# A graph network's third layer: the transposes and the projection of a group moved from two rounds to three rounds behind its sums

## The chip, the cores and the metric

The kernel runs on one core of one Trainium2 chip. The metric is the device time of one execution in microseconds; it was 6518.21 us before the change (median of 3 runs, 6515.67 to 6524.41). A core has several engines that work beside each other: TensorE (PE; its weight loads are PEld), VectorE (DVE), ScalarE (ACT), GpSimd (POOL) and SyncE (SP). Here SP issues most of the plain transfers and POOL issues the gathers.

## The reference, cut to what matters

There are 12500 nodes with 256 features each and 200000 edges, sorted by their target. Three layers of a graph network come first, then a layer norm, an attention over the same edges, and another layer norm.

```python
def _sage_layer(x, src, dst, inv_deg, W_self, W_neigh, b):
    agg = jax.ops.segment_sum(x[src], dst, num_segments=N_NODES)
    mean = agg * inv_deg[:, None]
    return x @ W_self + mean @ W_neigh + b
h = relu(_sage_layer(features, ...)); h = relu(_sage_layer(h, ...)); h = _sage_layer(h, ...)
x = _layernorm(x + h)                       # the end of the third layer: called z below
ZU = jnp.einsum('nd,kdr->knr', Z, U)        # the projection of z onto 4 heads of 16
# attention along the edges over ZU, one gradient step, relu
x = _layernorm(x + _L1_gnn_ref(x, ...))
```

The third layer differs from the first two: its rows are normalised, and each block of rows is also transposed (`zT`) and projected onto 64 columns (`zu`), since the attention reads `z`, its transpose and its projection.

## The kernel before

**Two ways of summing.** Most target nodes get their sums group by group. A group is 1792 edges; 76 groups in the third layer cover the first 8404 nodes. The rows of the sources are gathered into `xg` (14 gathers by POOL, line 838), split into a high and a low part in `hl` (ScalarE, line 858; VectorE, line 860), and multiplied on TensorE with a one-hot matrix `oh` (line 866). A further matmul (line 469) adds the sum carried over from the group before. The last 4096 nodes get their sums from a dense product instead: a matrix of edge counts (`c`, cast by ScalarE at line 749) with all rows (`hz`), in 392 steps of 8 matmuls 128x512 each (line 755, into `px`). Blocks of these nodes are ended in `end_block`. The dense steps are dealt out over the groups' rounds as `units`; about 5.7 fall to a round.

**A group's seven steps.** `group(g)` (line 820) is a Python generator, and each `next` writes out one step:

1. loads, gathers, one-hot matrix, the first half of the sums
2. the second half of the sums and the carry
3. the mean (ScalarE, line 908)
4. transposes of the own rows `hb` and of `mean` into `pT`, copied to `hT` (line 368)
5. eight products into `pO` (line 354) and `sage_end`: bias (line 344), residual (348), the layer norm (334 to 339), which writes `hn`. VectorE does all of it but one square root on ScalarE (337)
6. in the third layer alone, in `finish`: two transposes of `hn` into `pT` (line 363), copied to `zT` (368)
7. the projection into `pO` (line 374), its copy `zu` (376), a square and two small reductions for a bound (672 to 675), and three stores by SP of `zu`, `hn` and `zT` (line 440)

**What sets the order.** Lines 927 to 959 lay the steps out in rounds. A round has seven turns, `turns`: the newest group takes steps 1 and 2 in turns 2 and 5 (counted from 0), the group before it takes steps 3, 4 and 5 in turns 0, 3 and 6, and in the third layer the one before that, `old[0]`, takes steps 6 and 7 in turns 1 and 4. The dense units are spread between the turns. `chained` ties the matmul groups in that order: the first of a group comes after the last of the group before it. The matmuls between the first and the last of a group are not tied so, and a planner, which orders each engine's instructions, may place them earlier. The engines then take their instructions in the planned order.

So step 5 of a group is the last turn of one round, and step 6 of the same group is the second turn of the next round.

**Buffers.** `hn` has 3 buffers, `zT` 4, `xg` 3, `hl` 2, `c32` 3, `hz` 3, and `pT` and `pO` are one PSUM tile each, shared by all their users. `hn` is held from step 5 until its store in step 7.

Of the kernel before, what the change touches and what calls it, by code (L numbers as in the profile page):

```python
# [9 lines left out]
F32 = mybir.dt.float32  # L10
# [13 lines left out]
P = 128  # L24
# [24 lines left out]
def tile_gnn_resnorm(  # L49
# [14 lines left out]
    N, D = x.shape  # L64
# [7 lines left out]
    L = len(w_self)  # L72
# [115 lines left out]
    with tc.tile_pool(name="prep", bufs=1) as prep, \  # L188
# [78 lines left out]
        far = prep.tile([P, NG * GT], F32, name="far")  # L267
# [73 lines left out]
    def sage_end(wk, l, wts, po, hn, xb):  # L341

        n = po.shape[0]
        nc.vector.tensor_add(po, wts[2][:n], po)  # L344
        if l < L - 1:
            return nc.scalar.activation(hn, po, AF.Relu)
        y = wk.tile([n, D], F32, name="y")
        nc.vector.tensor_add(y, xb, po)
        return layernorm(wk, y, hn)
# [121 lines left out]
    def fast_sage():  # L471
        with ExitStack() as fx:
# [82 lines left out]
            def chained(first, last):  # L555
                if chain[0] is not None:
                    after(chain[0], first)
                chain[0] = last
# [4 lines left out]
            def count_ends(pool, n):  # L563
                for g in ends_of[counted[0]:n]:
                    row_ends(pool, g)
                    counted[0] += 1
# [214 lines left out]
            def due(l, g):  # L781
                sg, ahead = (SG, 0) if l else (SG0, G1)
                n, end = NDL[l] // sg * NQ, swept(l)
                if g >= end:
                    k = cuts[NDL[l]].NGS - LAG - end
                    return n + (2, 2, 4)[l] * sg * min(k, g + 1 - end) // k
                if l:
                    return n * (g + 1) // end

                n1 = n * 3 // 5  # L790
                return max(0, n1 * (g + 1 - G1) // (GB - G1) if g < GB else n - (n - n1) * (end - g - 1) // (end - GB))

            def built(g):
                if g < GA:
                    return max(0, g + 4 - GA)
                if g < G1:
                    return 3 + PER * (g + 1 - GA) // (G1 - GA)
                return min(BUILDS, 3 + PER + (BUILDS - PER - 3) * (g + 1 - G1) // (GB - G1))

            turn, H, summed = 0, GT // 2, []  # L800
            for l in range(L):
                table = x if l == 0 else hd[l - 1]
                W = (D + 2, D, D)[l]
                cut = cuts[NDL[l]]
# [3 lines left out]
                with ExitStack() as lx:  # L808
                    done, formed = 0, 0
                    lk = lx.enter_context(tc.tile_pool(name="layer", bufs=2))  # L810
# [9 lines left out]
                    def group(g):  # L820
# [94 lines left out]
                        yield  # L915
                        po, *mm = sage_products(ps, wts[l], hT)
                        chained(*mm)
                        hn = lk.tile([P, D], F32, name="hn", bufs=3)
                        sage_end(lk, l, wts[l], po, hn, xb)
                        tiles, made = yield from finish(l, lk, ps, hn, po, light)  # L920
                        store_rows(tiles, at[0], made, at[1])
# [2 lines left out]

                    live, rounds = [], 2 if l < L - 1 else 3
                    for g in range(cut.NGS + rounds - 1):
                        units, old = [], list(live)
                        if g < cut.NGS:  # L930
                            new = group(g)
                            live.append(new)
                            todo, more = due(l, g) - done, built(g) - formed if l == 0 else 0
                            done, formed = done + todo, formed + more
                            n = max(todo, more)
                            for i in range(n):
                                units += [forming] * ((i + 1) * more // n - i * more // n)
                                units += [steps_] * ((i + 1) * todo // n - i * todo // n)

                        late = old.pop() if old and g <= cut.NGS else None  # L940
                        turns = [late, old[0] if old else None, new if g < cut.NGS else None, late,
                                 old[0] if old else None, new if g < cut.NGS else None, late]
                        assert len(old) < 2
                        n = len(turns)
                        for i in range(n):
                            if turns[i] is not None:
                                next(turns[i])
                            if i == 2 and l == 0 and g < cut.NGS:

                                soon = min(NU, 1 + max(0, built(g + 1) - 3 + PER - 1) // PER) if built(g + 1) else 0  # L950
                                count_ends(tk, max(counted[0] + (1 if soon else needs[U0] // 2),
                                                   max((needs[u] for u in parts[:soon]), default=0)))
                                for _ in range(-(-NQ // ZB // (G1 - 2))):
                                    next(xsplit, None)
                            for u in units[len(units) * i // n:len(units) * (i + 1) // n]:
                                next(u, None)
                        if g >= rounds - 1:
                            live.pop(0)
                    assert not live
                    assert next(steps_, None) is None and (l or (next(forming, 0) == 0 and next(xsplit, 0) == 0))  # L960

            t1 = wp.tile([P, 1], F32, name="t1")
# [282 lines left out]
    with tc.If(ok > 0) as which:  # L1245
        fast_sage()
# [38 lines left out]
```

## Time and profile before

| what | value |
|---|---|
| median of 3 runs | 6518.21 us |
| the profiled execution: own time, span | 8272.62 us, 8270.8 us |
| busy in the span: PE, PEld, DVE, ACT, POOL | 5557.8, 4432.6, 3901.5, 3473.0, 4811.3 us |
| mean granted TensorE clock | 0.763 |
| first layer until about | 2290 us |
| second layer, first and last mean (line 908) | 2307.9, 3958.6 us |
| third layer, first and last mean | 4055.1, 5952.2 us |
| attention, from about | 5970 us to the end |

The profiled execution is an execution of its own and took 1754 us longer than the median. Times in the profile are counted from the first instruction. A line of groups or of the timeline names the line in the kernel, the engine, the operation, what is written and read, and how often; the idle time stands behind it, with what ended it. "remote" stands for a releaser that the profile could not name. Ends of matmuls are modelled.

### The profile page before, as it was taken

The page shows a single profiled execution, that of the slowest core. Times are in us where ns is not written, and L with a number is a line of the kernel's source. Part 1 is how long each engine was busy: PE and PEld are TensorE (multiplying, and loading weights), DVE is VectorE, ACT ScalarE, POOL GpSimd, SP SyncE. Part 2 cuts the span into 40 slices and gives each one's busy share as a digit, 9 for nine tenths or more (in the row PEclk, how much of TensorE's full clock was granted, in tenths as well). Part 3 has the DMA queues.
Part 4 walks back from the last instruction along what each step waited for, and adds up shares of the span by engine and source line. Part 5 has one row for each costly group of instructions (what it writes and reads, how often), then busy time and mean ns, then how long its engine had stood idle before and what let it go on. Part 6 is the DMA issues. An engine that isn't in the chain of part 4 may idle for free. (4 is left out here: it accounts for less than half of the span.)

```text
span 8270.8 us, 86872 instructions
## 1 busy us (share of the span) xinstructions
PE 5557.8 (67%) x23570; PEld 4432.6 (54%) x23570; DVE 3901.5 (47%) x9939; ACT 3473.0 (42%) x6309; POOL 4811.3 (58%) x4977
## 2 busy tenths in 40 slices
PE   4678787777678888887577777777544444444445
PEld 3556566555556666666465656566434333443344
DVE  4655545433434444444344545444445555555555
ACT  2333333344345454444344444444334444444444
POOL 5555555555566565565455555545366666666665
PEclk7888888888889998898788888889755555555555
DMA  7766666766566666665466656666333333333332
GB/s 207 244 203 217 220 225 223 226 214 218 178 195 217 208 214 207 206 213 178 156 190 184 192 178 191 185 181 195 108 86 88 88 94 88 88 89 88 91 91 67
DMA packets 896774, 1391.65 MB, mean 168 GB/s; under 512 B 191216, under 2 KB 540424, under 8 KB 892173
## 3 DMA queue, kind: packets, MB, share of 16 engines
q1 hardware_dynamic: 650511, 834.50, 31.3%
q0 software_dynamic: 213152, 496.65, 21.5%
q10 hardware_dynamic: 32606, 54.81, 1.9%
q8 instruction: 189, 3.10, 0.2%
q14 instruction: 316, 2.59, 0.1%
HBM read 1175.15 MB, written 210.33 MB: 168 GB/s over the span
## 5 line engine op out<-in xcount | busy, mean ns | idle before, releaser
L121 POOL DMA_INDIRECT xg<-h_d,srcI x2128 | 2082.3, 979 | 1645.5 <-issue 604.6
L755 PE MATMUL px<-c,hz 128*128 128x512 f32 x8232 | 2405.2, 433 | 266.6 <-issue 128.7
L121 POOL DMA_INDIRECT zs<-zu_d,srcI x1563 | 1495.9, 957 | 828.2 <-issue 416.8
L755 PEld LDWEIGHTS px<-c,hz 128*128 128x128 f32 x8232 | 1613.2, 203 | 646.0 <-issue 178.6
L749 ACT ACTIVATE c<-c 128x1024 fp32r<-128x1024 uint8 (+1 forms) x1274 | 1123.0, 893 | 1891.3 <-remote 692.8
L121 POOL DMA_INDIRECT xg<-in_x_dram,srcI x1218 | 1170.4, 961 | 925.0 <-PE pA L874 450.9
L462 DVE TENSOR_TENSOR oh<-rel,gconst 128x1792 fp32r<-128x1792 f32 (+1 forms) x354 | 714.2, 2018 | 1098.8 <-PE pO L382 312.1
L860 DVE TENSOR_TENSOR hl<-xg,hl 128x256 fp32r<-128x256 f32 x2128 | 780.2, 420 | 539.1 <-ACT hl L858 434.2
L1057 PE MATMUL pT<-ident,ag 128*64 128x128 f32 x112 | 47.2, 422 | 1157.3 <-DVE ag L392 625.5
L858 ACT ACTIVATE hl<-xg 128x512 fp32r<-128x512 f32 x1216 | 622.8, 569 | 266.3 <-PE pA L866 88.0
L1057 PEld LDWEIGHTS pT<-ident,ag 128*64 128x64 f32 x112 | 14.4, 129 | 1238.2 <-DVE ag L392 669.9
L866 PE MATMUL pA<-hl,oh 128*128 128x512 f32 x2128 | 625.3, 430 | 53.3 <-issue 51.0
L866 PEld LDWEIGHTS pA<-hl,oh 128*128 128x128 f32 x2128 | 432.9, 206 | 163.4 <-issue 59.8
L874 PE MATMUL pA<-xg,oh 128*128 128x258 f32 x1764 | 511.1, 451 | 3.8 <-DMA b<-in_L_gnn_b_dram 2.6
L874 PEld LDWEIGHTS pA<-xg,oh 128*128 128x128 f32 x1764 | 402.1, 233 | 94.7 <-issue 15.5
L645 ACT ACTIVATE win<-pc 128x392 uint16<-128x392 f32 x512 | 240.9, 495 | 459.6 <-PE pc L642 204.6
L344 DVE TENSOR_TENSOR pO<-b,pO 128x256 f32<-128x256 f32 x306 | 130.9, 428 | 639.8 <-remote 484.6
L354 PE MATMUL pO<-ws,hT 128*128 128x256 f32 x968 | 284.2, 419 | 171.4 <-DVE hs L661 50.5
L1027 DVE TENSOR_TENSOR zz<-zs,pD 128x896 f32<-128x896 f32 x224 | 242.2, 1082 | 328.7 <-remote 159.7
L1019 PE MATMUL pD<-z,ohT 128*128 128x128 f32 x1563 | 360.9, 418 | 53.3 <-DVE lg L1030 18.4
L633 DVE TENSOR_SCALAR oa<-iota,kt 128x128 bf16<-128x128 f16 x1024 | 268.9, 263 | 244.8 <-remote 86.6
L1019 PEld LDWEIGHTS pD<-z,ohT 128*128 128x128 f32 x1563 | 346.9, 333 | 54.1 <-issue 35.5
(257 smaller groups left out, 8112.4 us busy)
## 6 DMA issues: line engine op xcount, KB each, us to landing
hz<-hs_d SPq DMA_DIRECT2D x637, 512.0 KB
c<-cnt_d SPq DMA_DIRECT2D x112, 896.0 KB
ohT<-rel_d SPq DMA_DIRECT2D x111, 896.0 KB
hs_d<-hs SPq DMA_DIRECT2D x218, 256.0 KB
cnt_d<-win ACTq DMA_DIRECT2D x32, 1568.0 KB
xg<-h_d,srcI POOLq DMA_INDIRECT x2128
c<-cnt_d SPq DMA_DIRECT2D x70, 448.0 KB
zs<-zu_d,srcI POOLq DMA_INDIRECT x1563
```

Source lines behind the costliest of these rows:

```text
L121: return nc.gpsimd.indirect_dma_start(out=dst_ap, out_offset=None, in_=table, in_offset=bass.IndirectOffsetOnAxis(ap=idx, axis=0))
L354: mm = [nc.tensor.matmul(po, hT[:, i], wts[i // DC][:, i % DC], start=i == 0, stop=i == 2 * DC - 1) for i in range(2 * DC)]
L462: nc.vector.tensor_tensor(oh[:, :m], r[:, :m].unsqueeze(2).to_broadcast([P, m, P]), nodes.unsqueeze(1).to_broadcast([P, m, P]), op=op)
L633: nc.vector.tensor_scalar(oa[:, c], iota16[:, :P], kt[:, 0, at], None, op0=OP.is_equal)
L749: nc.scalar.activation(c32.rearrange("p (k d) -> p k d", d=P), c8[:, :, b % CB], AF.Copy)
L755: made.append(nc.tensor.matmul(px[f][i], hz[:, b % ZB, a:a + P].bitcast(F32R), c32[:, i * 512:(i + 1) * 512], start=b == 0 and part == 0, ...
L858: nc.scalar.activation(hi[:, b + j:b + j + n, :W], xg[:, a + j:a + j + n, :W], AF.Copy)
L860: nc.vector.tensor_tensor(lo[:, b + j, :D], xg[:, a + j, :D], hf[:, b + j, :D], op=OP.subtract)
L866: mm.append(nc.tensor.matmul(pa, oh[:, a + j], hl[:, j].rearrange("p i d -> p (i d)"), start=first, stop=stop))
L874: mm.append(nc.tensor.matmul(pa[:, :W], oh[:, a + j], xg[:, a + j, :W], start=first, stop=stop))
L1019: mm = [nc.tensor.matmul(pd[:, j * 2 * KR:(j + 1) * 2 * KR], ohT[:, a + j], z2.rearrange("p k i r -> p (k i r)"), start=True, stop=True) f ...
L1027: nc.vector.tensor_mul(zz, zg.unsqueeze(2).to_broadcast([P, n * K, 2, R]), pd[:, :n * 2 * KR].rearrange("p (m i r) -> p m i r", i=2, r=R))
```

## The change

In the third layer step 6 and step 7 are taken by the group three rounds behind the newest instead of two; `hn` gets a fourth buffer, as it is held one round longer. The list `live` now keeps all groups, and `late`, `far` and `now` are picked from it by number. The number of rounds stays: in the last round the two groups that are left take steps 6 and 7 one after the other. In the first two layers `far` is None, as `old[0]` was, and the turns come out as before.

```diff
-                        hn = lk.tile([P, D], F32, name="hn", bufs=3)
+                        hn = lk.tile([P, D], F32, name="hn", bufs=4)
...
-                    live, rounds = [], 2 if l < L - 1 else 3
-                    for g in range(cut.NGS + rounds - 1):
-                        units, old = [], list(live)
+                    live, lag = [], 1 if l < L - 1 else 3
+                    for g in range(cut.NGS + min(lag, 2)):
+                        units = []
                         if g < cut.NGS:
-                            new = group(g)
-                            live.append(new)
+                            live.append(group(g))
...
-                        late = old.pop() if old and g <= cut.NGS else None
-                        turns = [late, old[0] if old else None, new if g < cut.NGS else None, late,
-                                 old[0] if old else None, new if g < cut.NGS else None, late]
-                        assert len(old) < 2
+                        late = live[g - 1] if 0 < g <= cut.NGS else None
+                        far = live[g - lag] if l == L - 1 and g >= lag else None
+                        now = live[g] if g < cut.NGS else None
+                        turns = [late, far, now, late, far, now, late]
+                        if g > cut.NGS:
+                            turns = [far, far, live[-1], live[-1]]
                         n = len(turns)
...
-                        if g >= rounds - 1:
-                            live.pop(0)
-                    assert not live
+                    assert all(next(s, 0) == 0 for s in live)
```

## The prediction

> **What bounds the kernel now.** The change touches the third layer alone, so I first read the windows table for the second layer's and third layer's steady stretches (columns: stretch, length, then busy us and instructions of PE, PEld, DVE, ACT, POOL; then granted clock, DMA share, GB/s).
>
> ```profile
> 2330.00:3990.00 1660.00, 1364.06 (x5527) 1078.40 (x5526) 702.71 (x1629) 812.35 (x1390) 984.98 (x1010) 0.90 0.66 206
> 4075.00:5806.00 1731.00, 1316.10 (x5692) 1054.76 (x5693) 798.66 (x2155) 754.35 (x1265) 918.04 (x935) 0.88 0.62 186
> ```
>
> TensorE is busiest in both: 82% and 76%; POOL is at 53% and DMA at 62% in the third. Then the waits of the third layer (who waits for whom: us in total, times, longest) and its row for the transposes of `hn`:
>
> ```profile
> POOL xg L121 <- ACT hl L858: 459.9, 51, 16.8
> PE pT L363 <- DVE hn L339: 280.4, 36, 13.2
> ACT c L749 <- remote: 274.0, 43, 13.5
> DVE pO L344 <- remote: 273.5, 31, 11.9
> ```
>
> ```profile
> L363 PE MATMUL pT<-ident,hn 128*128 128x128 f32 x138 | 37.9, 367 | 304.0 <-DVE hn L339 280.4 <-DVE bn_rs L338 11.6 <-issue 11.1
> ```
>
> So 304 us of TensorE idleness end at the instruction that is moved. The timeline says how much of it the move can remove. First a common round (start, length, what; idle before it in brackets):
>
> ```profile
> 4712.91 1.03 PE L354 MATMUL pO<-wn,hT 128*128 128x256 f32 x4
> 4713.59 3.54 PE L755 MATMUL px<-c,hz 128*128 128x512 f32 x14
> 4714.08 1.42 DVE L860 TENSOR_TENSOR hl<-xg,hl 128x256 fp32r<-128x256 f32 x4
> 4715.42 0.42 DVE L344 TENSOR_TENSOR pO<-b,pO 128x256 f32<-128x256 f32 x1
> ...
> 4718.01 0.57 DVE L339 TENSOR_SCALAR hn<-y,bn_mv,bn_rs 128x256 f32<-128x256 f32 x1
> ...
> 4718.73 0.41 PE L363 MATMUL pT<-ident,hn 128*128 128x128 f32 x2 [0.69 <-DVE hn L339]
> ```
>
> The products end at 4713.94. VectorE is still in its L860 subtractions and takes up L344 1.48 us later; L344 to the end of L339 is 3.16. TensorE has 4.09 us of other matmuls and then idles 0.69. Now the other kind of round:
>
> ```profile
> 4807.91 1.03 PE L354 MATMUL pO<-wn,hT 128*128 128x256 f32 x4
> 4808.59 3.55 PE L755 MATMUL px<-c,hz 128*128 128x512 f32 x14
> ...
> 4819.27 0.43 DVE L344 TENSOR_TENSOR pO<-b,pO 128x256 f32<-128x256 f32 x1 [10.24 <-remote]
> ...
> 4822.34 0.69 PE L363 MATMUL pT<-ident,hn 128*128 128x128 f32 x2 [9.51 <-DVE hn L339]
> ```
>
> L344 waits for nothing but the products (and its queue), recorded as done at 4808.9, and starts 10.3 us later. Its own chain is as short as ever (3.01 us to the end of L339). The 9.51 us are thus TensorE's own lateness, seen at the next wait. Such spells (VectorE or ScalarE starting over 4 us after the recorded end of the matmul that it waited for alone) come in all three layers, 4 to 10 in every 250 us, 176 in all, also in the second layer, where no transposition of `hn` follows.
>
> **What the Trainium skill says.** "Perfetto Trace Analysis", Tensor Engine Instruction: a matmul's recorded end is computed from its size, "a model, not a measurement". The trace agrees (10.3 us above), so gaps in TensorE's row after such a spell aren't pure waits. "TensorE: Matmul & The Clock Gate", Step-by-step: matmuls stay in program order, only weight loads are pulled ahead; so a transpose that waits holds all that follows, as the gaps show. Same page, What's actually happening: after an idle window of about 3.4 us the clock halves. After the 9.51 us the trace grants 0.5 until 4828; the 0.69 us gap costs none.
>
> **The change, part by part.**
> Removed: the wait of L363 on `hn`. I read all 76 groups in the timeline. Of the 67 before 5806, 32 have no late products (L344 within 4.5 us of them): their gaps sum to 23.4 us, 0.73 each. By its parts: 1.5 us until L344 + 3.2 of chain - 4.0 of covering matmuls. 35 are of the late kind, 7.38 us each. For these I also credit 0.73, taking the rest as lateness that stays: 67 x 0.73 = 49 us. The last nine groups have no sweep matmuls to cover; leaving out the two with late products (10.2 and 13.2), seven gaps sum to 20.4. The very last group still waits: 2.72 us here,
>
> ```profile
> 5959.85 1.90 PE L354 MATMUL pO<-wn,hT 128*128 128x256 f32 x4
> 5964.47 0.41 PE L363 MATMUL pT<-ident,hn 128*128 128x128 f32 x2 [2.72 <-DVE hn L339]
> ```
>
> of which the group before it, now drained at this point, fills about 0.3 + 0.5 (two transposes, four projection matmul records). So the end gives 20.4 - 2.2 = 18 us.
>
> Moved, per group: two transposes and four projection records on TensorE (0.4 + 0.55), the `zT` copy (0.42, VectorE; ScalarE in the light last groups), the `zu` copy (0.22), ScalarE's square (0.25), two small reductions (0.22 + 0.16), and on SP the register load and three stores. All keep their turn in the round; they serve a group one older. None is added or dropped, so busy sums stand. SP's stores still wait for `zu`, and the `hz` loads stand behind them: the wait SPq L420 <- DVE zu L376 is 73 us in 31 times now and shouldn't grow, since `zu`'s inputs are ready no later. The other queues keep their order by turns; POOL's gathers are held by sums, which come slightly earlier.
>
> Fourth `hn`: no instruction. L339 reuses a tile whose store was issued in the same place as before (four groups back, stored one round later), so that spare time is unchanged; 1 KB more of each partition. Without it, L339 would wait for a store only one round old.
>
> Next to be late: `pT` is one PSUM tile. The `zT` copy must leave it before the `hT` transposes two turns on. In program order these stand behind 8 + 2 + 8 + 7 + 8 matmuls, some 7.5 us after the products; the copy, still behind the layernorm on VectorE, ends at 1.5 + 3.2 + 0.4 = 5.1. That leaves 2.4 us. The sums' last L860 end 1.6 us before `hn` does, so they return little. I take 5 us as returned.
>
> Sum: 49 + 18 - 5 = 62 us of the profiled execution, whose own time is 8272.6 us (span 8270.8). That is 1754 us over the median of 6518.2, about what 176 spells of 10 us make. So I take the runs shown as nearly free of spells, and the 62 us, all from rounds without one, unscaled. 6518 - 62 = 6456, say **6455**.
>
> **Bounds of the unknown.** Lower: nothing, if some other wait takes every gap. Upper: the recorded waits are real. The second layer does the same sums without `hn` transposes; by ScalarE's `mean` its round is 22.6 us against 25.9 here. About 0.95 of the difference is the transposes' and projection's own work: 2.35 x 67 = 157, and 18 at the end, 175 us; scaled by 6518/8271 it is 138: 6380.
>
> **Rivals.**
> A, likeliest (0.55): as above, 6455, its own range 6425 to 6495.
> B, the recorded waits are mostly real (0.14): 6380. For it: 280 us stand in the waits, and the slower rounds of the third layer. Against: the late L344.
> C, the wait moves (0.17): TensorE reaches the next L866 or the `hT` transposes sooner and waits there, or `c`'s casts (ACT c L749 <- PE px L755, 245 us) don't keep up. About 10 us remain, the unfilled end: 6508. Against: in undisturbed 4693 to 4760 TensorE's row is 91% busy.
> D, slower (0.14): the `zT` copy is queued on VectorE behind the next group's seven L860 (2.4 us and their wait for ACT L858). It then ends over 7.5 us after the products, and the `hT` transposes wait on `pT`. It decides from 8.2 us, where the 0.73 is eaten. With 9 us: (9 - 7.5 - 0.73) x 67 = 52, less 18 at the end: +34, 6552. For it: VectorE's order around here is set by a planner, not by turns alone. Against: the copy stands ahead of them in program order.
> The first two layers' turns come out the same, and the `hn` chain does leave TensorE's path, so "it does nothing" is only in C.
>
> **How the numbers follow.** 0.2% (13 us) is about what a measurement of this kernel can tell from no change. A and B are faster; C is within it for 0.11 and faster for 0.06; D slower. Faster 0.75, same 0.11, slower 0.14. Range 6375 to 6525: all of A and C, half of B and a little more (0.08), none of D: 0.80.
>
> **What would show it.** In the third layer, PE pT L363 <- DVE hn L339 falls from 280 us below 20, only the last group's being left. The round by `mean` shortens by 1 to 2.5 us; the second layer's stays. L363 <- DVE zT L368 on `pT` stays under 25 us (10 in PEld's row now); if it takes over, C or D. The profiled time falls by 60 to 180 us. I'd be wrong if the idle time before L363 just appears before L866, L354 or `px`, or if the unprofiled runs have these spells too (then B).

## The result, and the profile after

| | median | lowest to highest |
|---|---|---|
| before | 6521.31 us | 6513.86 to 6529.34 (6 runs) |
| after | 6488.75 us | 6485.75 to 6504.63 (6 runs) |

The ratio is 0.9955, with a 95% interval of 0.9941 to 0.997: 33 us faster between the medians (29 by the ratio), where 63 us were forecast. The profiled execution after took 6504.63 us (span 6502.8).

One thing has to be known to read the numbers: some sets of runs, profiled or not, took 8050 to 8290 us with the kernel before instead of 6514 to 6535, with the spells of late TensorE that the prediction met, and since the first profile of before (8272.62 us) was of this kind, "with spells" and "without" tell the two apart below, and each ratio is within one set.

The lines of before that follow are from a profile without spells (`e7_before`, 6535.29 us). They show three stretches of the third layer: from its first `mean` to the tenth later, from there to the 68th later, and on to the first gather of the attention. First before (windows: stretch, length, then busy us and instructions of PE, PEld, DVE, ACT, POOL, then granted clock, DMA share, GB/s):

```profile
3130.80:3312.50 181.70, 170.39 (x768) 138.62 (x768) 104.11 (x268) 109.77 (x179) 138.41 (x143) 0.97 0.80 252
3312.50:4380.30 1067.80, 1061.59 (x4992) 865.02 (x4991) 703.49 (x1909) 650.63 (x1110) 811.62 (x836) 1.00 0.85 266
4380.30:4519.90 139.60, 94.06 (x407) 77.44 (x405) 86.18 (x277) 54.09 (x139) 58.38 (x58) 0.81 0.40 115
```

And after:

```profile
3136.40:3320.10 183.70, 174.35 (x786) 141.66 (x786) 105.00 (x271) 108.71 (x178) 139.81 (x145) 0.98 0.81 253
3320.10:4374.40 1054.30, 1048.05 (x4965) 863.68 (x4966) 700.48 (x1903) 651.33 (x1109) 802.61 (x824) 1.00 0.86 267
4374.40:4490.60 116.20, 83.78 (x413) 70.38 (x411) 85.64 (x283) 52.89 (x140) 67.21 (x68) 0.85 0.55 152
```

The stretches change by +2.0, -13.5 and -23.4 us. In the long middle one TensorE is busy 99.4% of the time already before, so there is hardly a wait to remove. Over all three, TensorE's idle time falls by 15 us (63.1 to 48.0) and its busy time by 20 us (1326.0 to 1306.2), with the same instructions (6167 and 6164 matmul records). Half of the 20 us lies in the last stretch, where the granted clock rose from 0.81 to 0.85; the other half was not traced to a cause. The row of the moved transposes, before without spells and then after (count, busy, mean ns, idle before):

```profile
L363 PE MATMUL pT<-ident,hn 128*128 128x128 f32 x152 | 33.3, 302 | 44.6 <-DVE hn L339 44.1
```
```profile
L363 PE MATMUL pT<-ident,hn 128*128 128x128 f32 x152 | 29.5, 275 | 1.6 <-DVE hn L339 1.6
```

The wait is gone but for the last group's 1.6 us. It was 44.1 us before without spells, not the 304 us of idle time read with them. A common round before, without spells, in the timeline:

```profile
3665.89 1.03 PE L354 MATMUL pO<-wn,hT 128*128 128x256 f32 x4
...
3666.57 3.55 PE L755 MATMUL px<-c,hz 128*128 128x512 f32 x14
3666.96 0.43 DVE L344 TENSOR_TENSOR pO<-b,pO 128x256 f32<-128x256 f32 x1
...
3669.96 0.86 PE L866 MATMUL pA<-hl,oh 128*128 128x512 f32 x3
...
3670.33 0.41 DVE L339 TENSOR_SCALAR hn<-y,bn_mv,bn_rs 128x256 f32<-128x256 f32 x1
...
3670.80 0.44 PE L363 MATMUL pT<-ident,hn 128*128 128x128 f32 x2
```

(Lines of other instructions are left out at the dots.) The products end at 3666.92, L344 starts at 3666.96, `hn` is done at 3670.74, and TensorE, whose cover runs until 3670.82, goes on without a gap. The planner had put matmuls that belong behind the transposes (six of the next dense step, three of the next sums) ahead of them, just enough. The same place after:

```profile
3684.13 1.03 PE L354 MATMUL pO<-wn,hT 128*128 128x256 f32 x4
...
3684.81 2.19 PE L755 MATMUL px<-c,hz 128*128 128x512 f32 x8
3685.20 0.43 DVE L344 TENSOR_TENSOR pO<-b,pO 128x256 f32<-128x256 f32 x1
...
3686.84 0.38 PE L363 MATMUL pT<-ident,hn 128*128 128x128 f32 x2
...
3686.97 2.10 PE L755 MATMUL px<-c,hz 128*128 128x512 f32 x8
...
3688.57 0.41 DVE L339 TENSOR_SCALAR hn<-y,bn_mv,bn_rs 128x256 f32<-128x256 f32 x1
...
3688.91 1.79 PE L866 MATMUL pA<-hl,oh 128*128 128x512 f32 x7
```

Now the transposes stand 1.7 us before the next `hn` is even written (they read the older one), and the matmul groups stand whole, as the turns have them.

**What the layer ends on.** POOL's gathers of the third layer, before without spells and after (count, busy, mean ns, idle before):

```profile
L121 POOL DMA_INDIRECT xg<-h_d,srcI x1064 | 1037.5, 975 | 351.5 <-issue 132.0 <-DVE hl L860 56.5 <-DMA xg<-h_d,srcI 38.7
```
```profile
L121 POOL DMA_INDIRECT xg<-h_d,srcI x1064 | 1038.1, 976 | 355.4 <-issue 129.4 <-DVE hl L860 63.7 <-DMA xg<-h_d,srcI 31.4
```

From the first to the last they take 1363.2 us before and 1362.9 after: 1064 gathers, one after the other, 0.98 us each with about 0.30 between them, and hardly a gap over 0.6 us (three such gaps before, one after, 3 us and 1 us in all). The change to TensorE's waits did not shorten that. The two engines are close to each other here: a group's 14 gathers take 17.9 us (1363.2 / 76), while a round of the long middle stretch took 18.4 us before (1067.8 / 58) and 18.2 after. TensorE thus falls behind the gathers by less than half a microsecond a round. What the change shortened is how far the rest of the layer lags behind the last gather. POOL's timeline there, before without spells, then after:

```profile
4455.10 0.95 POOL L121 DMA_INDIRECT xg<-h_d,srcI  x1 [0.30 <-issue]
4519.94 0.94 POOL L121 DMA_INDIRECT zs<-zu_d,srcI  x1 [63.89 <-DVE gconst L456]
```
```profile
4460.96 1.10 POOL L121 DMA_INDIRECT xg<-h_d,srcI  x1 [0.30 <-issue]
4490.62 0.94 POOL L121 DMA_INDIRECT zs<-zu_d,srcI  x1 [28.56 <-DVE gconst L456]
```

63.89 - 28.56 = 35.3 us, against 33 us between the medians. The idle time in brackets is this lag.

### The profile page after: what moved, and what is told of

The parts are those of the page before. It is cut to its first block, busy times and chain, and to the rows that moved or that the text cites. A ratio compares the mean times of both kernels' runs of the same rounds, so it can differ in the third digit from the quotient of the medians.

```text
span 6502.8 us, 86803 instructions
## 1 busy us (share of the span) xinstructions
PE 5140.6 (79%) x23570; PEld 4209.6 (65%) x23570; DVE 3906.3 (60%) x9939; ACT 3473.9 (53%) x6309; POOL 4809.5 (74%) x4977
## 4 chain that ended last, share of the span: by engine, by line
PE 25%; POOL 10%; DMA 7%; DVE 5%; issue 5%; ACT 1%; DVEq 0%; POOLq 0%; SPq 0%; ACTq 0%
POOL zs L121 9%; PE px L755 9%; DMA zs<-zu_d,srcI 4%; PE pA L866 3%; DMA xg<-h_d,srcI 3%; PE pA L1042 3%; PE pD L1018 3%; PE pO L381 2%; PE pO L354 2%; PE pO L382 1%; DVE wf L1035 1%; DVE zz L1026 1%; DVE lg L1029 1%; PE pT L363 1%; PE pA L469 1%
## 5 line engine op out<-in xcount | busy, mean ns | idle before, releaser
L755 PE MATMUL px<-c,hz 128*128 128x512 f32 x8232 | 2255.5, 414 | 110.0 <-ACT c L749 83.5
L755 PEld LDWEIGHTS px<-c,hz 128*128 128x128 f32 x8232 | 1521.7, 191 | 427.8 <-ACT c L749 107.1
L860 DVE TENSOR_TENSOR hl<-xg,hl 128x256 fp32r<-128x256 f32 x2128 | 790.1, 419 | 578.5 <-ACT hl L858 575.4
L858 ACT ACTIVATE hl<-xg 128x512 fp32r<-128x512 f32 x1216 | 648.6, 571 | 612.9 <-DMA xg<-h_d,srcI 484.5
L866 PE MATMUL pA<-hl,oh 128*128 128x512 f32 x2128 | 574.7, 409 | 12.8 <-DVE hl L860 9.2
L866 PEld LDWEIGHTS pA<-hl,oh 128*128 128x128 f32 x2128 | 406.3, 193 | 108.5 <-DVE hl L860 13.8
L874 PE MATMUL pA<-xg,oh 128*128 128x258 f32 x1764 | 431.4, 397 | 6.1 <-ACT agg L910 3.4
L874 PEld LDWEIGHTS pA<-xg,oh 128*128 128x128 f32 x1764 | 343.7, 199 | 64.0 <-ACT agg L910 7.2
L1042 PE MATMUL pA<-w,oh 128*128 128x136 f32 x1563 | 361.3, 418 | 0.0
L1032 ACT ACTIVATE wf<-lg 128x28 f32<-128x28 f32 x224 | 50.5, 226 | 576.4 <-DVE lg L1029 575.2
L634 DVE TENSOR_SCALAR ob<-iota,kt 128x196 bf16<-128x196 f16 x1024 | 349.7, 344 | 0.0
```

The costliest lines, as they stand in the source:

```text
L634: nc.vector.tensor_scalar(ob[:, c], iota16[:, 1:1 + NQ * 2], kt[:, 1, at], kt[:, 2, at], op0=OP.is_equal, op1=OP.mult)
L755: made.append(nc.tensor.matmul(px[f][i], hz[:, b % ZB, a:a + P].bitcast(F32R), c32[:, i * 512:(i + 1) * 512], start=b == 0 and part == 0, ...
L858: nc.scalar.activation(hi[:, b + j:b + j + n, :W], xg[:, a + j:a + j + n, :W], AF.Copy)
L860: nc.vector.tensor_tensor(lo[:, b + j, :D], xg[:, a + j, :D], hf[:, b + j, :D], op=OP.subtract)
L866: mm.append(nc.tensor.matmul(pa, oh[:, a + j], hl[:, j].rearrange("p i d -> p (i d)"), start=first, stop=stop))
L874: mm.append(nc.tensor.matmul(pa[:, :W], oh[:, a + j], xg[:, a + j, :W], start=first, stop=stop))
```

## The experiments

Theory 1: the wait was smaller than read, and what was removed is gained. Theory 2: the wait was as large as read, and half of it turned up elsewhere.

**The kernel before, profiled three more times** (`e0_before`, `e5_before`, `e7_before`; no edit).

> The kernel before, unchanged, profiled a second time, since the first profile of it has spells of late TensorE and the profile after the change has none. Time as before, 6520 within 0.3%. Theory 1 (the wait was smaller than I read it): without spells the idle time of TensorE ended by hn at line 363 is 25 to 45 us in all, and the gain of about 32 us is that wait, with nothing given back. Theory 2 (the wait moved): that idle time is 60 us or more, and the profile after shows 25 us or more that was not there before, ahead of L866, the hT transposes, or the dense matmuls px that wait for their cast.

> The kernel before, for a profile on the same chip as these. As for its first profiling here: without spells, theory 1 expects 25 to 45 us of TensorE idle time ended by hn at line 363, theory 2 60 us or more.

> The kernel before, for a profile without spells, if this chip has none (median near 6520): theory 1 (the wait was smaller than I read it) expects 25 to 45 us of TensorE idle time ended by hn at line 363, theory 2 (it moved) 60 us or more. With spells (near 8100) it repeats the profiles there: 160 us or more.

`e0_before` took 8101.39 us and `e5_before` 8204.76: both with spells, with at least 161 and 239 us of waits for `hn` on TensorE. `e7_before` took 6535.29 without: 44.1 us, the upper edge of theory 1's span. The spells do not come from profiling: unprofiled runs of the same sets took 8053.99 to 8294.31 us.

**The fourth buffer alone** (`e1_hn4`).

```diff
-                        hn = lk.tile([P, D], F32, name="hn", bufs=3)
+                        hn = lk.tile([P, D], F32, name="hn", bufs=4)
```

> One part alone: hn has 4 buffers, the rounds stay as before. Both theories: ratio 1.000 within 0.002, since no instruction and no order differs. If it is faster by over 0.2%, the buffer and not the lag is the gain.

Ratio 0.9994 (0.9971 to 1.0018), with spells. Under these conditions the buffer by itself gives nothing that can be told; without spells it was not run alone.

**The body alone** (`e3_body_only` with spells, `e8_body_only` without). The edits from here on are against the changed kernel; `first_light` is the round in which the dense steps are used up.

```diff
-                        far = live[g - lag] if l == L - 1 and g >= lag else None
+                        first_light = swept(l)
+                        far = None
+                        if l == L - 1 and g >= (3 if g <= first_light else 2):
+                            far = live[g - (3 if g <= first_light else 2)]
...
+                        if l == L - 1 and g == first_light:
+                            turns = [late, far, now, late, far, live[g - 2], now, live[g - 2], late]
                         if g > cut.NGS:
-                            turns = [far, far, live[-1], live[-1]]
+                            turns = [far, far]
```

> The other part alone: three rounds until the dense steps are used up, there the two groups that are left take their steps in one round, then two rounds as before. Theory 1 (the wait was smaller than I read it, all of it gained): the change less the end's 8 to 18 us, so 14 to 24 us faster on a chip without spells of late TensorE. Theory 2 (the wait moved): the same time by another way; the traces tell it, by 25 us or more of new idle time in the body. On a chip with spells (median near 8100) the prediction's rival B expects 100 us or more from the body, its case A no more than 50.

> The body alone again. Without spells, theory 1: 14 to 24 us less (0.9963 to 0.9978); theory 2: the same. If it is the whole 30 us, the end gives nothing. With spells: 0.9795 as before, within 0.006.

Without spells 0.9986 (0.9979 to 0.9992): 9 us, under the 14 to 24 of both theories. With spells 0.9795 (0.9745 to 0.9845): 169 us of 8240, the 100 us or more that rival B expected.

**The end alone** (`e2_end_only` and `e6_end_only` with spells, `e9_end_only` without).

```diff
-                        far = live[g - lag] if l == L - 1 and g >= lag else None
+                        first_light = swept(l)
+                        far = None
+                        if l == L - 1 and g < first_light and g >= 2:
+                            far = live[g - 2]
+                        elif l == L - 1 and g > first_light:
+                            far = live[g - 3]
```

> One part alone: the lag of three rounds only in the last rounds of the third layer, from the round in which the dense steps are used up; until then two rounds as before (and 4 buffers of hn). By the prediction's terms the end is worth 18 us and the rest 49. Theory 1: 8 to 18 us faster (6502 to 6512), the end's share being as predicted and the body's mis-sized. Theory 2: also 15 to 18 us here, as the end has nothing that could take the wait. If it is under 5 us, the end was mis-sized, and the gain of 32 us is the body's.

> The end alone, as in the run before it that lay on a chip with spells. Without spells theory 1 and theory 2 both expect 8 to 18 us less (0.9972 to 0.9988); under 5 us the end was mis-sized.

> The end alone again. Without spells both theories: 8 to 18 us less (0.9972 to 0.9988); under 5 us, the end was mis-sized. With spells: 0.9983 as in both runs before, within 0.003.

Without spells 0.9961 (0.9947 to 0.9974): 25 us, more than either theory's 8 to 18. With spells 0.9984 (0.9958 to 1.0009) and 0.9983 (0.9953 to 1.0012): not told from nothing. So without spells the end is three quarters of the gain, and with them the body is about four fifths (169 of the 206 us that the whole change gives below). In the last stretch of `e9_end_only`, TensorE's busy time itself fell:

```profile
4375.70:4485.48 109.78, 83.64 (x407) 70.46 (x405) 83.78 (x278) 52.28 (x139) 57.56 (x58) 0.87 0.52 146
```

As many matmul records, 407, took 94.06 us before, at a granted clock of 0.81 instead of 0.87. So shorter waits are one part of what the end gives, and matmuls that take less time, 10 us in all, are another.

**The change once more, with spells** (`e4_after`).

> The change itself once more, on the chip of these runs. Without spells: 0.9955 as before, within 0.002. If this chip has spells (before near 8100): case A of the prediction, which leaves TensorE's lateness in place, expects 45 to 70 us less, 0.992 to 0.9945; rival B, in which the recorded waits are real where there are spells, 110 to 175 us, 0.979 to 0.987; and none at all if the lateness only shows at the next wait.

0.975 (0.9702 to 0.9797): 206 us less of 8240. That is rival B, and somewhat beyond its 175 us. The gathers show why. Before with spells (`e5_before`), then after with spells (`e4_after`):

```profile
L121 POOL DMA_INDIRECT xg<-h_d,srcI x1064 | 1040.3, 978 | 906.1 <-ACT hl L858 436.2 <-issue 257.9 <-DMA hs_d<-hs 45.3
```
```profile
L121 POOL DMA_INDIRECT xg<-h_d,srcI x1064 | 1038.1, 976 | 708.4 <-issue 295.8 <-ACT hl L858 136.4 <-DMA hs_d<-hs 47.2
```

There TensorE is so late that POOL waits for free `xg` tiles, 436 us behind the split of the rows. The gathers then take 1901 us from first to last before, 1699 after, while the lag behind the last one hardly moves (64.1 and 53.3 us). Here the gathers wait for TensorE, so its waits count. The waits of TensorE in the same two, before and after:

```profile
PE pT L363 <- DVE hn L339: 238.9, 33, 11.6
PE pO L714 <- DVE y L348: 30.1, 4, 9.9
```
```profile
PE pT L363 <- DVE zT L368: 54.8, 17, 7.1
PE px L363 <- DVE hnd L339: 30.7, 6, 18.4
PE pT L363 <- DVE hTd L368: 29.7, 10, 8.7
```

A part of the wait came back at the single `pT` tile, as the prediction had named it, but only here.

**The last dense blocks staggered, on top of the change** (`e10_end_blocks`). After the change TensorE's largest wait in the end was for `hnd`, 22.1 us.

```diff
-                    hn = lk.tile([P, D], F32, name="hnd")
+                    hn = lk.tile([P, D], F32, name="hnd", bufs=4 if l == L - 1 else None)
...
-                    for d in range(0, sg, len(banks)):
-                        blocks = [end_block(k0, d + i, aggT, bank) for i, bank in enumerate(banks)]
-                        for _ in range(parts_of):
-                            for block in blocks:
-                                next(block)
-                                yield
+                    sets = [[end_block(k0, d + i, aggT, bank) for i, bank in enumerate(banks)]
+                            for d in range(0, sg, len(banks))]
+                    if l == L - 1 and len(banks) > 1:
+                        order = [s for k in range(len(sets) + 1)
+                                 for s in (sets[k:k + 1] + sets[max(k - 1, 0):k]) * 2]
+                    else:
+                        order = [blocks for blocks in sets for _ in range(parts_of)]
+                    for blocks in order:
+                        for block in blocks:
+                            next(block)
+                            yield
```

> On top of the change: the last eight dense blocks, whose hnd transposes hold TensorE for 22 us in the end of the changed kernel, take their steps staggered too, two blocks' first steps between the other two's normalisation and transposes (hnd with 4 buffers). If the end is a chain of such waits on TensorE, as theory 1 has it, 10 to 20 us less than the change: 0.9925 to 0.994 of before on a chip without spells. If the end is bound by something else, for one the pO tile that the blocks now hold longer, the ratio stays at 0.9955 within 0.0015 or is worse. With spells: 0.965 to 0.975.

0.9949 (0.9936 to 0.9963), not told from the change's 0.9955; the 10 to 20 us that theory 1 expected did not come. The wait for `hnd` did vanish from TensorE. In its place TensorE waits for the sums' own inputs (the first figure is us, then times and the longest; line numbers are five higher here):

```profile
PE pA L871 <- DVE hl L865: 7.8, 6, 3.3
PE pA L871 <- DVE bn_mv L335: 6.9, 1, 6.9
```

**Four rounds instead of three** (`e11_lag4`).

```diff
-                        hn = lk.tile([P, D], F32, name="hn", bufs=4)
+                        hn = lk.tile([P, D], F32, name="hn", bufs=5)
...
-                    live, lag = [], 1 if l < L - 1 else 3
+                    live, lag = [], 1 if l < L - 1 else 4
...
-                            turns = [far, far, live[-1], live[-1]]
+                            turns = [far, far, live[-2], live[-2], live[-1], live[-1]]
```

> A lag of four rounds with 5 buffers of hn, three groups drained in the last round. Theory 1: nothing of the wait is left for a fourth round to hide, so 0.9955 within 0.0015 without spells, 0.975 within 0.006 with them. If the gain grows with the lag (more than 0.002 better), it isn't the wait for hn but the looser order that pays. The drain could cost 1 to 3 us.

0.9947 (0.9933 to 0.9961): again not told from the change.

**All six kernels without spells, side by side.** The gather stream and the time from its end to the attention's first gather, both from POOL's timeline in one profile of each kernel:

| kernel | gathers, first to last | from there to the attention | less than before | measured gain |
|---|---|---|---|---|
| before | 1363.2 us | 63.9 us | | |
| body alone | 1362.4 | 51.3 | 12.6 | 9 (5 to 14) |
| end alone | 1360.2 | 34.9 | 29.0 | 25 (17 to 35) |
| the change | 1362.9 | 28.6 | 35.3 | 29 (20 to 38) |
| and blocks staggered | 1362.7 | 29.8 | 34.1 | 33 (24 to 42) |
| four rounds | 1367.1 | 26.6 | 37.3 | 35 (25 to 44) |

The gains are the ratios with their intervals, times the median of before in the same set of runs. The stream is 1360 to 1367 us in all six, and each gain is, within its interval, what the end behind the last gather became shorter. The second layer agrees: it has no transposes of `hn`, and its 1064 gathers take 1358 to 1363 us in the same six profiles. No run changed the gathers themselves, so that their pace is the limit is read from these streams and not tested.

In the changed kernel the last group's `mean` comes 11.7 us after the last gather (42.2 before), which leaves little to win there. Neither theory was right. Theory 1 had the size of the wait, but not that all of it is gained: TensorE's waits for `c` rose from 3.3 to 14.8 us over the layer and those for `hnd` from 10.8 to 22.1, so about 23 of the 42.5 us that were removed came back. Theory 2 expected such a return, but from a wait of 60 us or more. That the end still comes 35 us sooner is made up by TensorE's busy time, which fell by 20 us.

## Why the prediction was wrong

**The body's term, 49 us: the step that failed.** It failed twice: the wait was mis-sized, and what a removed wait is worth was taken from the wrong bound.

*Its size.* The waits for `hn` ahead of the end are 11.2 + 5.5 = 16.7 us (the first and the second stretch), 0.25 a round and not 0.73. The part that was wrong is the 1.5 us until L344: without spells its median over the 67 rounds is 0.04 us (`e7_before`), and in the round shown above the matmuls in between cover the chain to within some hundredths of a microsecond. The rounds that the prediction took as undisturbed were rounds of a profile with spells; in the one it shows, VectorE still had L860 subtractions to do when the products were ready. That an earlier spell had put it behind is likely, but not shown.

*What it is worth: the bound.* The prediction took TensorE for the bound and POOL, 53% busy, for free. Both figures came from a profile with spells. Without them POOL gathers without a break through the whole layer (1363 us for 1064 gathers at 1.28), 17.9 us a group, and TensorE at 18.4 us a round is only a little slower. So a gain in the body is worth only what it takes off TensorE's lag behind the gathers: at most 27 us over the 58 middle rounds (an estimate: 1067.8 less 58 rounds of gathers at 17.94). The row of busy shares hid it, because the 0.30 us between gathers count as idle. And the 11.2 us of the first ten rounds bought nothing. TensorE's waits there, before and after:

```profile
PE pT L363 <- DVE hn L339: 11.2, 5, 4.1
PE px L755 <- ACT c L749: 3.3, 1, 3.3
```
```profile
PE px L755 <- ACT c L749: 11.1, 7, 2.1
```

ScalarE's casts `c` share its queue with the splits of the rows, and these wait longer for gathers (ACT hl L858 <- DMA xg goes from 39.5 to 68.8 us in that stretch). So the wait moved to the casts, as rival C has it, though they were held by the gathers and not by TensorE. Measured alone, the body gave 9 us.

**The end: right in kind, 18 forecast, 25 measured.** The prediction left out two groups with late products. Without spells these two wait 2.0 and 6.0 us, and all nine 27.4 in the waits view; 1.6 stay, which makes 25.8. That this is so near the measured 25 is in part luck: at the end of the changed kernel 11.3 us came back as waits for `hnd`, and 10.3 us were gained in busy time, which the prediction held to be unchanged. There is also a slip in the sum: the seven gaps in that profile (0.28, 3.21, 5.99, 0.95, 3.00, 2.72, 2.72) add up to 18.9 and not 20.4, and 2.72 less 0.8 is 1.9 and not 2.2, so the term should have read 17.

**"5 us returned": mis-sized.** About 23 us came back without spells, at `c` (7.8 of the 11.5 us in the first ten rounds) and at `hnd`, neither of which is in the sum. The `pT` tile, for which the 5 us stood, held: no wait of size there without spells. With spells it took 54.8 us.

**The spells.** That the runs compared were free of them was right. But it doesn't follow that the rounds of a disturbed profile without late products are like rounds of an undisturbed run, and the 49 us rested on that. The other assumption, that the waits after late products aren't removed, was wrong too: under spells the change gives 206 us, and the comparison with the second layer, used for rival B (175 us in that profile), was the better estimate for those conditions. That a matmul's recorded end is a model (the Trainium skill, "Perfetto Trace Analysis", Tensor Engine Instruction) agrees with the 10.3 us in the prediction, but it didn't tell that the gap behind it was worthless.

**Direction and moved parts: right, with one exception.** The busy times of VectorE (3910.0 and 3906.3 us) and POOL (4807.3 and 4809.5) stood, TensorE's did not. The buffer cost nothing that could be told, the wait for `hn` fell to 1.6 us, and rival D didn't come. The round by `mean` was to shorten by 1 to 2.5 us; it shortened by 0.2 in the long middle stretch. The median of 6488.75 lies within the range and in case A's own, near its edge, but not by A's reasoning: A's largest term gave 9 us instead of 49, and its end gave more than forecast.

## What to carry to other kernels

Before counting the waits of the busiest engine, ask for each other stream whether it runs without a break: work that is issued with a fixed pause between pieces is full at 76% "busy", and then only the lag behind its last piece can be won. Look at where each engine stands when that stream ends, not at the sum of waits before it, and compare the busy times too: a removed wait can come back elsewhere, or the work beside it can get shorter. And hold the profiled execution's own time against the runs: where they differ by a quarter, the profile shows another regime than the one that is measured, and its waits mustn't be priced for it.

## What the runs showed of the hardware

The same program took 8136 us (median of 35 runs) in one set of runs and 6523 (25 runs) in another, with no difference in the kernel. Under the slower conditions VectorE can start far after the recorded end of the matmuls that it waits for, 10.3 us in the round that the prediction shows. Waits at L344 with a releaser that the profile could not name come to 273.5 us, 31 times, in the third layer of the first profile of before (the line is in the prediction); `e7_before` has no such wait in any line. The attention, from its first gather to the end, takes 2294 us (`e5_before`) against 2014 (`e7_before`) too. The experiments with spells ran on two chips and those without on two others, and no chip is known to have shown both. Whether the chip or something else sets these conditions stays open.

Gathers issued back to back keep their pace whatever the load on TensorE was in these runs: 1.28 us each in the second and the third layer of all six kernels without spells.

TensorE's matmuls at the end of the layer took 94.06 us at a mean granted clock of 0.81 (`e7_before`) and 83.64 us at 0.87 (`e9_end_only`), with 407 records each.
